# A hybrid attention kernel: last block's chain in halves, centred weights, two batches' residual kept by channels and added on GpSimd, run-up of 10 tokens

## The chip, the cores and the metric

The kernel runs on one core of a Trainium2 chip. A core has a matrix engine (TensorE, PE in the profile; PEld is its weight load), a vector engine (VectorE, DVE), a scalar engine (ScalarE, ACT), GpSimd (POOL), and SyncE (SP), which here only starts transfers (DMAs). The metric is device time in microseconds (us), lower is better; the figure for a kernel is the median over its runs.

## The reference

Four images (B = 4) of 128 channels (C) and 64 x 64 = 4096 tokens (N), in single precision. Layer 0 is an attention between tokens with 64-wide projections. Layer 1 normalizes each token, attends causally over 128 channels, adds the result, and then runs a recurrence over the tokens whose result is added once more. Cut to what the change touches:

```python
t = t + attention(layernorm(t))              # causal
# feed-forward part, on layernorm(t):
Wx = layernorm(t) @ W.T                      # (B, T, H)
Wx = (Wx - mean) * rsqrt(var + eps) * gamma + beta   # mean, var over all B*T tokens
y = 0
for each token:                              # lax.scan over T
    y = sigmoid(Wx[token] + y @ V.T)
    ys[token] = y
t = t + ys
```

The mean and variance of the batch norm are taken over all tokens of all images, so the recurrence can't start before the last block's Wx is there.

## The kernel before, in words

A first function, `fast_path`, does the work in a form that is valid under two conditions, which it checks at its end; a flag then decides whether a second, general path runs. On these inputs it is not meant to run.

**The main part.** Tokens are taken in blocks of 512 (BLK; NB = 8 blocks in an image), keys in tiles of 128. For each block and layer, a list of *items* is written out, an item being two tiles of keys: scores on PE into `s_ps` (L835 for layer 0, L844 for layer 1), exponential on ACT into `p` (L849, L851), sums for the denominator on DVE into `dsum` (L873, L875), and the weighted sum of values on PE into `acc` (L895, L903). A loop over *slots* issues in each slot the scores of one item, the values of the item two before, and one *task* from a list of waiting tasks: chains of small steps that finish a block are written as generators, which yield how many slots later their next step falls due. So the order on every engine is that of the slots.

**A block's end in layer 1** is the generator `finish1`. `first` divides by the denominators and adds to the residual stream `xs` (`joined`, L624), stores the resulting tokens in `x2` in DRAM, tokens by channels (L740), and takes mean and variance per token (`moments`: L633, L634, L636, and a power on GpSimd, L638). `norm` improves the inverse root by one Newton step (`newton`, L462 to L468) and normalizes (L645). `second` brings the normalized block into a layout with channels on partitions: for most blocks by a DVE transpose in squares of 32 (L659) and DMAs through DRAM (`by_c`, eventually `xhT`), for the very last block by PE transposes (L653) and one DVE copy (L654). `third` multiplies by W into `wx_ps` (L769), takes the statistics for the batch norm (L772) and copies the result over the block in `xs` (L782; L779 for the last block), arranged by steps of the recurrence.

**The last block of the last image** has its own order, since no other work lies beside it: all its steps follow in adjacent slots, and some matmuls without a use (`warm`, L730) are put between them. The function `form_half`, early in the kernel, prepares half of V's row sums (`v_half`, L486 to L489) right after `form` has prepared a product of weights `g1` (L491 to L494). Both take their PSUM tile from `misc`, a pool of two tiles that small products share.

**The recurrence.** The 4096 tokens of an image are cut into 256 chunks (NCH) of 16 tokens (STEPS), and all chunks run side by side as columns of one matmul. A chunk doesn't know the state that the chunk before it ends with; instead, it starts some tokens earlier (WARM = 11, the *run-up*) from a guess, so that its state at its first token is close to the true one. At the end the states at which run-ups ended are compared with the true ends of the chunks before (`gap`, L1109 to L1114, limit TOL = 1e-6). In each of the 11 + 16 steps, and for each of the four images: a matmul with V on PE (`y_ps`, L1077), a scale-and-add of Wx on DVE (`z`, L1079), and a sigmoid on ACT (L1082). The first of the run-up's steps needs no matmul: it is one activation with scale and `shift_half` (L1074). Scale and shift come from a chain of small operations on 128 x 1 tiles, L1036 to L1046.

**The output.** `x2` is loaded again into `xr` by 8 DMAs (L1033), with chunks on partitions. After the last step, `residual` transposes the states on PE into `yT_ps` (L1096), adds them to `xr` on DVE (L1098; four tokens of 128 chunks at a time, 32 in all), and stores 512 KB after each second addition (L1100, 16 DMAs). The states of the first four steps are kept in `early`; those of later steps lie in `xs`, in place of Wx.

Of the kernel before, what the change touches and what calls it, by code (L numbers as in the profile page):

```python
# [15 lines left out]
P = 128  # L16
BLK = 512
CHUNK = 1024
LN_EPS = 1e-5
BN_EPS = 1e-5  # L20


@with_exitstack
def general_path(
# [14 lines left out]
    out: bass.AP,  # L39
# [243 lines left out]
    with tc.tile_pool(name="wx", bufs=1) as wxp, tc.tile_pool(name="fwork", bufs=3) as wk:  # L283
# [28 lines left out]
        with tc.tile_pool(name="ys", bufs=3) as ysp, tc.tile_pool(  # L312
# [13 lines left out]
            for kb in range(nblk):  # L326
                ps = nxt
                y = ysp.tile([P, STEPS, B], F32, tag="y", name="y")
                for t in range(STEPS):
                    if prev is not None:  # L330
                        nc.tensor.matmul(
                            ps[:, t, :], lhsT=vf, rhs=prev, start=False, stop=t == STEPS - 1, skip_group_check=True
                        )
                    nc.scalar.activation(y[:, t, :], ps[:, t, :], AF.Sigmoid)
                    prev = y[:, t, :]
                    if t == STEPS // 2 and kb + 1 < nblk:
                        nxt = preload(kb + 1)
                o = ysp.tile([P, B, STEPS], F32, tag="o", name="o")
                nc.gpsimd.tensor_tensor(o, xs[:, :, ts(kb, STEPS)], y.rearrange("p t b -> p b t"), ALU.add)
                op = ps_o.tile([P, B, P], F32, tag="o", name="oT_ps")  # L340
                for b in range(B):
                    nc.tensor.transpose(op[:, b, :], o[:, b, :], ident)
                oT = ysp.tile([P, B, P], F32, tag="oT", name="oT")
                nc.vector.tensor_copy(oT, op)
                nc.sync.dma_start(out=out[:, ts(kb, STEPS), :].rearrange("b n c -> n b c"), in_=oT)
# [4 lines left out]
def fast_path(  # L350
# [15 lines left out]
    out: bass.AP,  # L366
# [14 lines left out]
    WARM, TOL, STEPS = 11, 1e-6, 16  # L381
# [14 lines left out]
    x2 = dram.tile([B, N, P], F32, name="x2")  # L396
# [40 lines left out]
    vf = const.tile([P, P], F32, name="vf")  # L437
    gamma = const.tile([P, 1], F32, name="gamma")
# [10 lines left out]
    ends = const.tile([P, 9], F32, name="ends")  # L449
# [3 lines left out]
    v_half = const.tile([P, 1], F32, name="v_half")  # L453
    spare = const.tile([P, 1], F32, name="spare")

    def rsqrt(y, var, z):

        nc.gpsimd.tensor_tensor(y, var, mhalf[:, : y.shape[-1]], ALU.pow)
        newton(y, var, z)

    def newton(y, var, z, pinned=False):
# [4 lines left out]
        nc.vector.tensor_tensor(z, z, var, ALU.mult)  # L466
        nc.vector.tensor_scalar(z, z, -0.5, 1.5, ALU.mult, ALU.add)
        nc.vector.tensor_tensor(y, y, z, ALU.mult)  # L468

    with tc.tile_pool(name="batch", bufs=1) as batch, tc.tile_pool(name="rows", bufs=2) as rowp, tc.tile_pool(  # L470
# [15 lines left out]
        def form_half():  # L486
            hp = misc("h_ps")
            nc.tensor.matmul(hp[:, 0:1], lhsT=vf, rhs=point5, start=True, stop=True)
            nc.vector.tensor_copy(v_half, hp[:, 0:1])  # L489
# [91 lines left out]

        def folded(den, by_pe):
# [7 lines left out]
            if by_pe:  # L590
# [4 lines left out]
                nc.vector.tensor_tensor(own, dp.rearrange("p (q j) -> p q j", q=Q), quarter, ALU.mult)  # L595
# [32 lines left out]
        def moments(b, g):  # L628
# [10 lines left out]
            return mv, var, y  # L639

        def normed(b, g, dst, mv, var, y, pinned=True):

            newton(y, var, stat.tile([P, TPB], F32, tag="z", name="ln_z"), pinned)
            for j in range(TPB):
                nc.vector.tensor_scalar(  # L645
# [75 lines left out]
        def finish1(b, g):  # L721
# [4 lines left out]
            def warm(n, rhs):  # L726

                ps = ps_s.tile([P, 2 * BLK], F32, tag="s", name="warm_ps")
                for _ in range(n):
                    nc.tensor.matmul(ps[:, : BLK // 2].rearrange("p (a c) -> p a c", c=P) if len(rhs.shape) == 3 else ps[:, : BLK // 2], lhsT=ident, rhs=rhs, start=True, stop=True)  # L730

            def first():
# [5 lines left out]
                if final:  # L738
                    warm(9, agg[:, : BLK // 2])
                nc.sync.dma_start(  # L740
                    out=x2[b, ts(g, BLK)].rearrange("(j p) c -> p j c", p=P),
                    in_=xs[:, b, ts(g, BLK)].rearrange("p (j c) -> p j c", c=P),
                )
# [3 lines left out]
            def norm():  # L747
                normed(b, g, mem["xh"], *mem["of"], not final)

            def second():  # L750
                mem["xhT"] = wk.tile([P, BLK], F32, tag="xhT2", name="xhT2")
                if final:
                    transposed(mem["xh"], mem["xhT"], "xh2T_ps", nc.vector.tensor_copy)
                    warm(1, mem["xh"][:, 2:])
# [11 lines left out]

            def third():
                wp = misc("wx_ps")
                nc.tensor.matmul(wp, lhsT=wf, rhs=mem["xhT"], start=True, stop=True)  # L769
                if b == B - 1 and g == NB - 1:  # L770
                    in_range(True)
                nc.vector.bn_stats(ends[:, 3:] if final else stats[:, b * NB + g], wp)  # L772
# [3 lines left out]

                to = xs[:, b, ts(g, BLK)]
                if final:
                    nc.scalar.copy(to.rearrange("p (s c) -> p s c", c=CPB), wp.rearrange("p (c s) -> p s c", s=STEPS))  # L779
                    warm(6, to[:, : BLK // 2])  # L780
                else:
                    nc.scalar.copy(  # L782
                        to.rearrange("p (s j q u) -> p s j q u", q=Q, j=TPB, s=STEPS),
                        wp.rearrange("p (q j u s) -> p s j q u", q=Q, j=TPB, s=STEPS),
                    )
# [13 lines left out]
            yield 2, second  # L799
            yield 1 if final else 6 if g < 2 or g == NB - 1 else 4, third  # L800
# [84 lines left out]
        def values(it):  # L885
# [24 lines left out]
            if it.last:  # L910
# [8 lines left out]
                else:  # L919
                    bt.agg = wk.tile([P, BLK], F32, tag="agg", name="agg")  # L920
                    nc.scalar.copy(bt.agg, bt.acc[:, 0])
# [102 lines left out]
    with tc.tile_pool(name="xr", bufs=1) as xrp, tc.tile_pool(name="y", bufs=2) as yp, tc.tile_pool(  # L1024
        name="ps_y", bufs=1, space=PSUM
    ) as ps_y, tc.tile_pool(name="ps_r", bufs=4, space=PSUM) as ps_r:

        HALVES = NCH // P
        by_chunk = lambda t: t.rearrange("b (h q s) c -> b h q s c", q=P, s=STEPS)
        xr = xrp.tile([P, B, HALVES, STEPS, P], F32, name="xr")  # L1030
        for b in range(B):
            for h in range(HALVES):
                nc.sync.dma_start(out=xr[:, b, h], in_=by_chunk(x2)[b, h])  # L1033
# [3 lines left out]
        scale = xrp.tile([P, 1], F32, name="scale")  # L1037
        var = xrp.tile([P, 1], F32, name="var")
        nc.vector.tensor_scalar(var, mv[:, 1:2], BN_EPS, None, ALU.add)
        rsqrt(scale, var, xrp.tile([P, 1], F32, name="z"))  # L1040
        nc.vector.tensor_tensor(scale, scale, gamma, ALU.mult)
        shift = xrp.tile([P, 1], F32, name="shift")
        nc.vector.tensor_tensor(shift, mv[:, 0:1], scale, ALU.mult)
        nc.vector.tensor_tensor(shift, beta, shift, ALU.subtract)
        shift_half = xrp.tile([P, 1], F32, name="shift_half")
        nc.vector.tensor_tensor(shift_half, shift, v_half, ALU.add)  # L1046
# [9 lines left out]

        assert HALVES * TPB == NB
        early = xrp.tile([P, B, TPB, NCH], F32, name="early")
        late = xs.rearrange("p b (r h k q) -> p b k r h q", h=HALVES, r=TPB, q=P)

        def states(b, s):
            return pair(early[:, b, s]) if s < TPB else late[:, b, s // TPB - 1, s % TPB]

        def step(b, s):

            wx = by_step[:, b, s % STEPS]
            if s == -1:
# [7 lines left out]
            else:  # L1075
                ps = ps_y.tile([P, NCH], F32, tag=f"y{b}", name="y_ps")
                nc.tensor.matmul(ps if s < 1 else pair(ps), lhsT=vf, rhs=prev[b], start=True, stop=True)  # L1077
# [4 lines left out]
                nc.scalar.activation(y, z if s < 0 else pair(z), AF.Sigmoid, bias=shift)  # L1082
            prev[b] = start[:, b, :NCH] if s == -1 else y

        for s in range(-WARM, STEPS):
            for b in range(B):
                step(b, s)

        def residual(b):

            for h in range(HALVES):
                for s0 in range(0, STEPS, TPB):
# [4 lines left out]
                    t = xr[:, b, h, ds(s0, TPB)]  # L1097
                    nc.vector.tensor_tensor(t, t, ps, ALU.add)  # L1098
                    if s0 % (2 * TPB):
                        nc.sync.dma_start(out=by_chunk(out)[b, h, :, part], in_=xr[:, b, h, part])  # L1100

        for b in range(B - 1):
# [4 lines left out]
        for b in range(B):  # L1107
            ps = ps_y.tile([P, NCH], F32, tag=f"y{b}", name="gap_ps")
            nc.tensor.matmul(pair(ps), lhsT=ident, rhs=prev[b], start=True, stop=False)  # L1109
# [72 lines left out]
```

## Time and profile before

| | us |
|---|---|
| median of the runs | 2064.52 (2064.33 to 2066.47, three runs) |
| profiled execution | 2065.22 |
| its span | 2063.5 |
| granted TensorE clock | 0.999 of full |
| main part, up to the last accumulation | 0 to 1974 |
| last block's chain and batch norm | 1974 to 1988 |
| recurrence | 1988 to 2036.6 |
| additions and output | 2036.6 to 2063.5 |

The span is what the profiler sees from the first to the last instruction; the execution's own time is 1.7 us longer. A line of the timeline gives the start, the length of the group (both in us), the engine and line, the operation with output and inputs and their shapes, how often it was run in the group, and in brackets how long the engine was idle before and which instruction ended that. A float32 matmul shows as two passes, so a count of 12 is six matmuls.

### The profile page before, as it was taken

The page shows a single profiled execution, that of the slowest core. Times are in us where ns is not written, and L with a number is a line of the kernel's source. Part 1 is how long each engine was busy: PE and PEld are TensorE (multiplying, and loading weights), DVE is VectorE, ACT ScalarE, POOL GpSimd, SP SyncE. Part 2 cuts the span into 40 slices and gives each one's busy share as a digit, 9 for nine tenths or more (in the row PEclk, how much of TensorE's full clock was granted, in tenths as well). Part 3 has the DMA queues.
Part 4 walks back from the last instruction along what each step waited for, and adds up shares of the span by engine and source line. Part 5 has one row for each costly group of instructions (what it writes and reads, how often), then busy time and mean ns, then how long its engine had stood idle before and what let it go on. Part 6 is the DMA issues. An engine that isn't in the chain of part 4 may idle for free.

```text
span 2063.5 us, 30798 instructions
## 1 busy us (share of the span) xinstructions
PE 2046.0 (99%) x11716; PEld 896.4 (43%) x11716; DVE 1492.2 (72%) x2865; ACT 990.1 (48%) x1071; POOL 135.5 (7%) x221
## 2 busy tenths in 40 slices
PE   9999999999999999999999999999999999999998
PEld 3333354444333345444333335544433334544456
DVE  4899867455889986644679987754588998764578
ACT  5666633323666643333466663332366664333365
POOL 1000011000000001000000001100000001100000
PEclk9999999999999999999999999999999999999999
DMA  4111012220100111231011101222000111110044
GB/s 113 43 23 23 12 42 51 69 67 16 57 8 17 23 28 46 62 77 41 17 43 22 23 12 42 47 67 72 16 17 5 19 23 28 41 43 25 16 169 165
DMA packets 207148, 89.03 MB, mean 43 GB/s; under 512 B 140960, under 2 KB 189600, under 8 KB 205968
## 3 DMA queue, kind: packets, MB, share of 16 engines
q1 hardware_dynamic: 205984, 86.42, 16.4%
q8 instruction: 94, 1.54, 0.3%
q14 instruction: 62, 0.51, 0.1%
q0 software_dynamic: 288, 0.39, 0.1%
q10 hardware_dynamic: 720, 0.16, 0.0%
HBM read 45.84 MB, written 36.89 MB: 40 GB/s over the span
## 4 chain that ended last, share of the span: by engine, by line
PE 97%; DVE 1%; issue 1%; DMA 0%; ACT 0%; POOL 0%; DVEq 0%; POOLq 0%; ACTq 0%
PE s_ps L844 22%; PE acc L903 22%; PE s_ps L835 22%; PE acc L895 21%; PE o_ps L614 3%; PE y_ps L1077 2%; PE r_ps L577 1%; PE wx_ps L769 1%; PE kr_ps L520 1%; PE v_ps L532 1%; DVE xr L1098 1%; PE warm_ps L484 0%; DMA swap<-kr 0%; ACT p L849 0%; DMA out_x<-xr 0%
## 5 line engine op out<-in xcount | busy, mean ns | idle before, releaser
L875 DVE TENSOR_TENSOR dsum<-dsum,p 128x1024 f32<-128x1024 f32 x676 | 826.0, 1222 | 430.2 <-ACT p L851 312.3
L849 ACT ACTIVATE p<-s_ps,nshift 128x1024 f32<-128x1024 f32 x512 | 569.6, 1117 | 315.0 <-PE s_ps L835 304.4
L851 ACT ACTIVATE p<-s_ps 128x1024 f32<-128x1024 f32 (+2 forms) x288 | 274.5, 953 | 605.5 <-PE s_ps L844 603.2
L895 PE MATMUL acc<-p,v 64*64 64x512 f32 x4096 | 529.2, 590 | 0.0
L835 PE MATMUL s_ps<-swap,kr 64*64 64x512 f32 x2048 | 524.1, 591 | 2.5 <-ACT p L849 1.6
L835 PE MATMUL s_ps<-kr 64*64 64x512 f32 x2048 | 524.1, 591 | 0.0
L844 PE MATMUL s_ps<-rows,xhT 128*128 128x512 f32 (+3 forms) x1152 | 502.9, 559 | 0.0
L903 PE MATMUL acc<-p,xh 128*128 128x512 f32 (+3 forms) x1152 | 500.8, 557 | 0.0
L903 PEld LDWEIGHTS acc<-p,xh 128*128 128x128 f32 x1152 | 216.2, 190 | 244.3 <-issue 233.5
L844 PEld LDWEIGHTS s_ps<-rows,xhT 128*128 128x128 f32 x1152 | 213.8, 190 | 242.4 <-issue 204.6
L895 PEld LDWEIGHTS acc<-p,v 64*64 64x64 f32 x4096 | 155.5, 133 | 281.7 <-issue 269.8
L835 PEld LDWEIGHTS s_ps<-swap,kr 64*64 64x64 f32 x2048 | 139.6, 133 | 141.1 <-issue 125.2
L835 PEld LDWEIGHTS s_ps<-kr 64*64 64x64 f32 x2048 | 139.7, 133 | 138.0 <-issue 133.8
L638 POOL TENSOR_TENSOR ln_rstd<-ln_var,mhalf 128x4 f32<-128x4 f32 x64 | 89.4, 1397 | 1102.1 <-DVE ln_var L636 1102.1
L883 DVE TENSOR_TENSOR dsum<-dsum,p 128x256 f32<-128x256 f32 (+1 forms) x120 | 54.9, 493 | 66.8 <-POOL p L855 66.8
L624 DVE SCALAR_TENSOR_TENSOR xs<-o_ps,recs,xs 128x128 f32<-128x128 f32 x256 | 75.0, 341 | 3.8 <-PE o_ps L614 0.5
L645 DVE TENSOR_SCALAR xh<-xs,ln_mv,ln_rstd 128x128 f32<-128x128 f32 x256 | 71.4, 342 | 2.2
L855 POOL TENSOR_SCALAR_AFFINE_SELECT p<-p 128x128 f32<-128x128 f32 x128 | 35.4, 300 | 466.6 <-ACT p L851 451.8
L633 DVE BATCH_NORM_STATS2 ln_st<-xs 128x6 f32<-128x128 f32 x256 | 63.3, 270 | 0.0
L782 ACT COPY xs<-wx_ps 128x512 f32<-128x512 f32 x31 | 18.1, 585 | 74.6 <-DVE stats L772 68.4
L873 DVE COPY dsum<-p 128x1024 f32<-128x1024 f32 x60 | 41.0, 684 | 12.1 <-ACT p L851 7.8
L1079 DVE SCALAR_TENSOR_TENSOR z<-xs,scale,y_ps 128x256 f32<-128x256 f32 x104 | 46.8, 480 | 2.9 <-PE y_ps L1077 1.7
(138 smaller groups left out, 984.6 us busy)
## 6 DMA issues: line engine op xcount, KB each, us to landing
xs<-in_xT SPq DMA_DIRECT2D x32, 256.0 KB, 2.9
by_r<-sqT SPq DMA_DIRECT2D x128, 64.0 KB, 2.2
xhT<-by_r SPq DMA_DIRECT2D x128, 64.0 KB, 2.0
x<-xs SPq DMA_DIRECT2D x32, 256.0 KB, 2.3
xr<-x SPq DMA_DIRECT2D x8, 1024.0 KB, 12.6
out_x<-xr SPq DMA_DIRECT2D x16, 512.0 KB, 4.7
by_c<-sqT SPq DMA_DIRECT2D x124, 64.0 KB, 1.8
xhT<-by_c SPq DMA_DIRECT2D x31, 256.0 KB, 2.6
```

The costliest lines, as they stand in the source:

```text
L614: nc.tensor.matmul(op[:, ts(j, P)], lhsT=agg[:, ts(j, P)], rhs=wv1 if layer else wo2, start=True, stop=True)
L624: nc.vector.scalar_tensor_tensor(t, in0=op[:, ts(j, P)], scalar=rec[:, j : j + 1], in1=t, op0=ALU.mult, op1=ALU.add)
L633: nc.vector.bn_stats(st[:, j], xs[:, b, ds(g * BLK + j * P, P)])
L638: nc.gpsimd.tensor_tensor(y, var, mhalf, ALU.pow)
L645: nc.vector.tensor_scalar(dst[:, j], xs[:, b, ds(g * BLK + j * P, P)], mv[:, j, 0:1], y[:, j : j + 1], ALU.subtract, ALU.mult)
L835: nc.tensor.matmul(ps[c * M : c * M + M, off : off + n], lhsT=bs[it.b].kr[part, h, ds(t % (NT // 2) * P + c * M, M)], rhs=rows[h], start=True,
L844: nc.tensor.matmul(ps[:, off : off + n], lhsT=lhsT, rhs=rhs, start=True, stop=True)
L849: nc.scalar.activation(it.p[:, :off], ps[:, :off], AF.Exp, bias=nshift)
L851: nc.scalar.activation(it.p[:, :off], ps[:, :off], AF.Exp, scale=float(P) ** -0.5)
L875: nc.vector.tensor_tensor(flat, flat, it.p, ALU.add)
L895: nc.tensor.matmul(bt.acc[h * M : h * M + M, r], lhsT=bt.v[part, t % (NT // 2), t // (NT // 2)], rhs=it.p[part, o : o + n], start=it.first ...
L903: nc.tensor.matmul(bt.acc[:, 0, q0:], lhsT=bt.xh[:, t], rhs=it.p[:, o : o + n], start=it.first and h == 0, stop=it.last and h == 1,)
```

## The change

- **Centred weights.** A matrix `center` (identity minus 1/128) times W gives `wfc`, whose product with a token doesn't depend on the token's mean. It is made in `form_half`, with a third PSUM tile from `misc` (`c_ps`). The last block is then only multiplied by its inverse root, and its mean isn't subtracted. `v_half` becomes `beta_half`, with beta added.
- **Halves.** For the last block the copy of `acc`, the normalization, the copy after the transposes, the product with W, the statistics and the copy into `xs` are done in two halves, some on ACT and some on DVE. An added dependency keeps the denominator's first operation behind DVE's half of the copy of `acc`.
- **Newton and scale chain.** The Newton step takes three operations instead of four, with -var/2 as an input; the scale and shift chain after the power takes fewer operations.
- **Two images by channels.** For images 0 and 1 (BY_C = 2) the residual stream isn't stored by tokens (`x2t` is for images 2 and 3 only). A new step `kept` transposes each of their blocks in squares on DVE and stores it by four DMAs in `x2c`, with channels on rows; it comes one slot after `second`. At the end `x2c` is loaded into `xc` (8 DMAs) and `x2t` into `xr` (4 DMAs).
- **Sums on GpSimd.** For these two images, after each of the 16 steps the states are added to `xc` by one GpSimd operation (128 x 512) and stored by one DMA of 256 KB (`out_c`). The kernel's output holds these images by channel, step and chunk, and the host puts them in order. `residual` runs for images 2 and 3 only.
- **Run-up.** WARM is 10 instead of 11, TOL 2e-6 instead of 1e-6.

```diff
-    WARM, TOL, STEPS = 11, 1e-6, 16
+    WARM, TOL = 10, 2e-6
...
-    def newton(y, var, z, pinned=False):
+    def newton(y, half, z, pinned=False):
         ins = nc.vector.tensor_tensor(z, y, y, ALU.mult)
...
-        nc.vector.tensor_tensor(z, z, var, ALU.mult)
-        nc.vector.tensor_scalar(z, z, -0.5, 1.5, ALU.mult, ALU.add)
-        nc.vector.tensor_tensor(y, y, z, ALU.mult)
+        nc.vector.tensor_tensor(z, z, half, ALU.mult)
+        nc.vector.scalar_tensor_tensor(y, in0=z, scalar=1.5, in1=y, op0=ALU.add, op1=ALU.mult)
...
             hp = misc("h_ps")
             nc.tensor.matmul(hp[:, 0:1], lhsT=vf, rhs=point5, start=True, stop=True)
-            nc.vector.tensor_copy(v_half, hp[:, 0:1])
+            nc.vector.tensor_tensor(beta_half, hp[:, 0:1], beta, ALU.add)
+            cp = misc("c_ps")
+            nc.tensor.matmul(cp[:, :P], lhsT=center, rhs=wf, start=True, stop=True)
+            nc.vector.tensor_copy(wfc, cp[:, :P])
...
+                if last:
+                    t = xs[:, b, ds(g * BLK + j * P, P)]
+                    if j % 2:
+                        nc.scalar.activation(dst[:, j], t, AF.Copy, scale=y[:, j : j + 1])
+                    else:
+                        nc.vector.tensor_scalar(dst[:, j], t, y[:, j : j + 1], None, ALU.mult)
+                    continue
...
-                    transposed(mem["xh"], mem["xhT"], "xh2T_ps", nc.vector.tensor_copy)
-                    warm(1, mem["xh"][:, 2:])
+                    for k, copy in enumerate((nc.vector.tensor_copy, nc.scalar.copy)):
+                        ps = misc("xh2T_ps")
+                        for i in range(2):
+
+                            nc.tensor.transpose(ps[:, ts(i, P)], mem["xh"][:, 2 * k + i], ident)
+                        copy(mem["xhT"][:, ts(k, BLK // 2)], ps[:, : BLK // 2])
...
+            def kept():
+
+                sq = squares(xs[:, b, ts(g, BLK)].rearrange("p (j c) -> p j c", c=P))
+                to = x2c[b, g].rearrange("r c (j q t) -> r c j q t", q=Q, t=S)
+                for q in range(Q):
+                    nc.sync.dma_start(
+                        out=to[:, :, :, q].rearrange("r c j t -> r (c j) t"),
+                        in_=sq[ts(q, S)].rearrange("r c j t -> r (c j) t"),
+                    )
...
+                to = xs[:, b, ts(g, BLK)].rearrange("p (s c) -> p s c", s=STEPS)
+                if final:
+                    in_range(True)
+                    for k in range(2):
+                        wp = misc("wx_ps")[:, : BLK // 2]
+                        nc.tensor.matmul(wp, lhsT=wfc, rhs=mem["xhT"][:, ts(k, BLK // 2)], start=True, stop=True)
+                        nc.vector.bn_stats(ends[:, 3 + 6 * k : 9 + 6 * k], wp)
+                        nc.scalar.copy(to[:, :, ts(k, CPB // 2)], wp.rearrange("p (c s) -> p s c", s=STEPS))
+                    warm(6, xs[:, b, ds(g * BLK, BLK // 2)])
+                    return
...
-                    nc.scalar.copy(bt.agg, bt.acc[:, 0])
+                    if it.b == B - 1 and it.g == NB - 1:
+                        nc.scalar.copy(bt.agg[:, : BLK // 2], bt.acc[:, 0, : BLK // 2])
+                        copied.append(nc.vector.tensor_copy(bt.agg[:, BLK // 2 :], bt.acc[:, 0, BLK // 2 :]))
+                    else:
+                        nc.scalar.copy(bt.agg, bt.acc[:, 0])
...
+        nc.gpsimd.tensor_tensor(y, var, mhalf[:, :1], ALU.pow)
+        nc.vector.tensor_scalar(half, var, -0.5, None, ALU.mult)
+        nc.vector.tensor_scalar(nmean, mv[:, 0:1], -1.0, None, ALU.mult)
+        nc.vector.scalar_tensor_tensor(z, in0=y, scalar=half, in1=y, op0=ALU.mult, op1=ALU.mult)
+        nc.vector.scalar_tensor_tensor(y, in0=z, scalar=1.5, in1=y, op0=ALU.add, op1=ALU.mult)
+        nc.vector.tensor_tensor(scale, y, gamma, ALU.mult)
+        nc.vector.scalar_tensor_tensor(shift_half, in0=nmean, scalar=scale, in1=beta_half, op0=ALU.mult, op1=ALU.add)
+        nc.vector.scalar_tensor_tensor(shift, in0=nmean, scalar=scale, in1=beta, op0=ALU.mult, op1=ALU.add)
...
+        def add(s):
+
+            t = sums.tile([P, BY_C, NCH], F32, tag="sum", name="sum")
+            by_grid = lambda t: t.rearrange("p b (g c) -> p b g c", c=CPB)
+            ins = nc.gpsimd.tensor_tensor(by_grid(t), by_step[:, :BY_C, s], by_grid(xc[:, :, :, s]), ALU.add)
+            tc.keep_in_program_order(ins)
+            tc.keep_in_program_order(nc.sync.dma_start(out=out_c[:, :, s].rearrange("b c k -> c b k"), in_=t))
...
         for s in range(-WARM, STEPS):
             for b in range(B):
                 step(b, s)
+            if s >= 0:
+                add(s)
...
-        for b in range(B - 1):
+        for b in range(BY_C, B - 1):
             residual(b)
```

The warming matmuls are also pinned to their place in the program's order (`keep_in_program_order`), and `warm` is called with 9 and 6 as before, the single one in `second` being left out.

## The prediction

> **What bounds the kernel now.** I read the shares by engine first, then the chain that ended last, then busy time by stretch, then the timeline of the tail. The page's share and chain:
>
> ```profile
> PE 2046.0 (99%) x11716; PEld 896.4 (43%) x11716; DVE 1492.2 (72%) x2865; ACT 990.1 (48%) x1071; POOL 135.5 (7%) x221
> ...
> PE 97%; DVE 1%; issue 1%; DMA 0%; ACT 0%; POOL 0%; DVEq 0%; POOLq 0%; ACTq 0%
> ```
>
> PE sets the time, but 99% is a mean. By stretch (columns: length, then busy us of PE, PEld, DVE, ACT, POOL, then granted clock, DMA share, GB/s):
>
> ```profile
> 30.00:1974.00 1944.00, 1942.38 (x11172) 827.32 (x11170) 1407.92 (x2668) 922.93 (x935) 127.97 (x198) 1.00 0.15 34
> 1974.00:1988.00 14.00, 10.87 (x48) 7.82 (x49) 8.10 (x42) 3.45 (x6) 1.66 (x3) 1.00 0.27 97
> 1988.70:2036.60 47.90, 47.90 (x220) 33.66 (x220) 46.78 (x105) 47.53 (x105) 0.00 (x0) 1.00 0.35 147
> 2036.60:2056.00 19.40, 17.65 (x135) 15.03 (x133) 19.32 (x35) 2.44 (x10) 0.00 (x0) 1.00 0.91 360
> ```
>
> Up to 1974 PE has no gap: other engines' work is free there, and only what holds PE costs. From 1974 to 1988 nobody is full: a serial chain (last block, then batch norm's scale). From 1988.7 the recurrence runs; DVE's scale-and-add (L1079) is 98% busy and each sweep of four batches takes four of them. From 2036.6 DVE's additions of the residual and the output DMA are both full. The timeline of those stretches:
>
> ```profile
> 1984.41 0.59 ACT L779 COPY xs<-wx_ps 128x512 f32<-128x512 f32 x1 [8.29 <-DVE ends L772]
> ...
> 1985.05 2.86 PE L730 MATMUL warm_ps<-xs,ident 128*128 128x256 f32 x12 [1.41 <-ACT xs L779]
> ...
> 1986.81 0.16 DVE L1046 TENSOR_TENSOR shift_half<-shift,v_half 128x1 f32<-128x1 f32 x1
> 1987.21 2.08 ACT L1074 ACTIVATE y<-xs,shift_half,scale 128x256 f32<-128x256 f32 x4 [2.21 <-DVE shift_half L1046]
> ...
> 1988.01 4.29 PE L1077 MATMUL y_ps<-y,vf 128*128 128x256 f32 x18
> ...
> 2036.52 14.43 DVE L1098 TENSOR_TENSOR xr<-xr,yT_ps 128x512 f32<-128x512 f32 x24
> ...
> 2037.82 18.46 SPq L1100 DMA_DIRECT2D out_x<-xr x16
> ```
>
> The warming matmuls (L730) end at 1987.91, the first y_ps starts at 1988.01: 1.04 after shift_half ends (1986.97). The recurrence's 104 scale-and-adds take 47.88 us (1988.72 to 2036.60): **0.460 each**, 1.84 a sweep. An addition takes 14.43/24 = 0.60; 32 last until 2055.92, and the last transfers and the drain need 7.6 more, to 2063.5.
>
> [...] GpSimd's power takes 1.01 us in the quiet tail and 1.91 beside L875, which adds two SBUF tiles (below). L1079 reads one SBUF tile and one PSUM tile, as L624 does, beside which an affine select took 294 ns, the same as alone.
> - [...] Here it fell about 4.5 us after PE's last work (2054.3); which shorter gap suffices isn't shown.
>
> ```profile
> 1941.07 1.91 POOL L638 TENSOR_TENSOR ln_rstd<-ln_var,mhalf 128x4 f32<-128x4 f32 x1 [23.96 <-DVE ln_var L636]
> ...
> 1978.39 1.01 POOL L638 TENSOR_TENSOR ln_rstd<-ln_var,mhalf 128x4 f32<-128x4 f32 x1 [7.04 <-DVE ln_var L636]
> ```
>
> **The change part by part** (line numbers of before, in us).
>
> 1. *Centred weights.* form_half gains a third PSUM tile (c_ps) in a pool of two. It waits until DVE has read the first, g_ps:
>
> ```profile
> 38.02 0.28 PE L488 MATMUL h_ps<-point,vf 128*128 128x1 f32 x2
> 38.12 1.23 DVE L875 TENSOR_TENSOR dsum<-dsum,p 128x1024 f32<-128x1024 f32 x1 [1.24 <-ACT p L849]
> 38.23 0.65 PE L835 MATMUL s_ps<-swap,kr 64*64 64x512 f32 x2
> ...
> 39.26 0.28 DVE L494 COPY g<-g_ps 128x128 f32<-128x128 f32 x1
> ```
>
> That copy stands behind an addition and ends at 39.54. In PE's built order s_ps and all that follows stand behind c_ps: 39.55 - 38.3 is 1.2, the matmul 0.2: **+1.4** on the bound engine. From 0 (other work is issued first) to +1.6.
>
> 2. *Chain of the last block.* Halving the copy of agg on ACT and DVE gains only 0.2: in the built order DVE's half waits for ACT's. Newton has one operation less: 0.2. From xh's start to the end of bn_stats is 4.15 now (1980.23 to 1984.38); with two xh each on ACT and DVE, copy, wx and statistics in halves, I work out 2.95: 0.65 until xh, 0.2 more for the transposes, 0.45 copy, 0.6 wx, then the second half's 0.6 wx and 0.4 statistics, partly overlapped: 1.2. After the batch norm's power there are 4 operations of 0.195 instead of 8: 0.8. Shift_half comes **2.4 earlier**, at 1984.55 (bounds 1.5 to 3).
>
> 3. *What the chain then meets.* In ACT's built order the first activation stands ahead of the two copies of wx into xs. The warming matmuls wait for both copies, and the first y_ps stands behind these matmuls on PE. Now the copy (1984.41) and the warming (1985.05) run under the scale chain; then they run after it: shift_half + 0.24 + 0.52 activation + 0.70 two copies + 0.05 + 2.96 matmuls = shift_half + 4.47, against + 1.04 now. First y_ps at 1984.55 + 4.47 = 1989.0 against 1988.0: **+1.0**. The chain's 2.4 is lost, and 1.0 more; the operations behind y_ps on every engine are the recurrence itself, so it all starts later by that. Bounds: -2.4 if the copies go first, +3.9 if in PE's 4 us without work (wx to warming) the clock halves, which doubles the 12 warming passes of 0.24.
>
> 4. *Run-up 10 for 11*: one sweep less, 4 x 0.460: **-1.84**.
>
> 5. *Keeping two batches' residual by channels.* Per block of batches 0 and 1, a DVE transpose (0.71 by L659) and four 64 KB DMAs take the place of one of 256 KB: 11.4 us of DVE and some 64 x 0.63 - 16 x 0.38 = 34 of SP, over 1,000 us. The cover is PE's matmuls; DVE has slack in each slot (10.98 of 12 us in a late stretch of layer 0). 0, bounds 0 to +2, if SP's longer queue delays a by_c or by_r whose reader PE is.
>
> 6. *Reading it back.* 12 DMAs instead of 8 for the same 8.4 MB; the first waits only for the last accumulation, as the last block's store does, which now stands behind it on SP. Even at half the full rate (400 GB/s in the tail) that ends by 2015, with the by-channel half (first in the queue) by 2000, ahead of the first sum (2009) and additions (2038). 0.
>
> 7. *Sums on GpSimd.* [...] one per sweep of 1.84: they lie beside the recurrence, with 256 KB written per sweep (142 GB/s). The last waits for batch 1's last sigmoid, ahead of the last scale-and-add[...]. Its store stands ahead of all the others' on SP, but the first of those has its two additions only 1.3 after: 0.
>
> 8. *After the recurrence.* 16 additions instead of 32: 16 x 0.60 + 0.6 (gap matmuls) = 10.2, then 7.6 as now: 17.8 from the last scale-and-add to the end, against 2063.5 - 2036.6 = 26.9: **-9.1**. By DMA: 4.45 MB at 400 GB/s is 11.1, and with start and drain 17.1, so DVE binds narrowly; -9.8 to -8.
>
> Sum: 1.4 + 1.0 - 1.84 - 9.1 = **-8.5**: span 2063.5 - 8.5 = 2055.0. Around the span lie 1.7 (the profiled execution took 2065.22), and that execution stands 0.7 over the median, 2064.52. So the median is **2056.0**.
>
> **Rivals.**
> - *The chain's gain arrives* (copies and c_ps cost nothing): -2.4 + 0 - 1.84 - 9.1 = -13.3, 2051.2. For it: everything PE waits for is short. Against: both waits follow from orders and buffers in the built program. In part (one of the two): 2053 to 2054.5. 12% for the two.
> - *The clock halves in PE's gap*: 12 x 0.24 = 2.9 more: 2058.9. [...] 18%.
> - *Main part disturbed by item 5*, +2 to +3: 2058.5. For: SP gets longer; against: PE's waits over the main part now sum to 1.6. 12%.
> - *GpSimd becomes the bound* (the slower side): if a sum takes d, the recurrence's last 16 sweeps end 16 x (d - 1.84) late; break-even at d = 1.84 + 8.5/16 = 2.37. [...] 7%.
> - *It doesn't do what it says*: the run-up of 10 misses the limit and the general path runs, far slower. The largest root gap worked out on the inputs is 1.0e-6, against 2e-6. 1%.
>
> The forecast's own case keeps 50%.
>
> **How the numbers follow.** Forecast 50%, faster rivals 12%, clock 18%, disturbed 12%, slower 8%. All but the last lie over 0.2% (4.1 us, about what a measurement can tell) below 2064.5, except that combined delays of item 5 and the clock may end within it: faster 0.84, same 0.08, slower 0.08. The range, 2050.8 to 2061.5, takes in the faster rival and the two delays together.
>
> **What would show it.** Right: y_ps first at about 1990.4 and after shift_half by 4.5; [...] 100 scale-and-adds of 0.46; 16 additions; 17.8 from the last one of the former to the end; one PE wait of 1.2 near 38. Wrong: GpSimd full from 2009 on, scale-and-adds longer than 0.46, or PE waiting on by_c or v.

## The result, and the profile after

The changed kernel takes **2059.45 us** in the median (2058.42 to 2060.53, nine runs), the kernel before, run beside it, 2064.71. The ratio is 0.9971, with an interval of 0.9962 to 0.9979: faster by 0.29%. The forecast was 2056.0, with a range of 2050.8 to 2061.5.

The page's shares by engine hardly differ, since the main part fills them:

```profile
PE 2039.1 (99%) x11646; PEld 909.0 (44%) x11646; DVE 1486.6 (72%) x2862; ACT 988.8 (48%) x1071; POOL 137.5 (7%) x237
```

By stretch, they differ at once (columns: length, busy us of PE, PEld, DVE, ACT, POOL, then clock, DMA share, GB/s):

```profile
1974.30:1985.00 10.70, 7.20 (x36) 5.67 (x36) 7.33 (x41) 2.93 (x6) 1.66 (x3) 1.00 0.83 191
1985.00:1992.00 7.00, 5.54 (x13) 3.93 (x13) 0.19 (x2) 2.61 (x6) 0.00 (x0) 0.54 1.06 204
1992.90:2039.00 46.10, 46.10 (x212) 32.69 (x211) 44.70 (x101) 44.99 (x100) 23.30 (x16) 1.00 0.56 189
2039.00:2050.40 11.40, 9.48 (x70) 8.29 (x68) 9.80 (x19) 2.39 (x10) 1.30 (x1) 1.00 0.85 330
```

The second line is new: 7 us in which DVE works 0.19, ACT 2.61, and PE is busy at a clock of 0.54. Of the recurrence only its first step, the activations that need no matmul, and the very first y_ps matmul fall into it. The last line is what was 19.4 long. The timeline of the changed kernel shows what fills the second line:

```profile
1984.84 0.22 DVE L1117 SCALAR_TENSOR_TENSOR shift_half<-nmean,scale,beta_half 128x1 f32<-128x1 f32 x1
...
1985.22 0.60 ACT L1150 ACTIVATE y<-xs,shift_half,scale 128x256 f32<-128x256 f32 x1 [3.61 <-DVE shift L1118]
1985.72 0.62 ACT L827 COPY xs<-wx_ps 128x256 f32<-128x256 f32 x2
1986.24 1.59 ACT L1150 ACTIVATE y<-xs,shift_half,scale 128x256 f32<-128x256 f32 x3
...
1986.40 5.49 PE L765 MATMUL warm_ps<-xs,ident 128*128 128x256 f32 x12 [3.78 <-ACT xs L827]
...
1991.94 6.38 PE L1153 MATMUL y_ps<-y,vf 128*128 128x256 f32 x26
...
1992.92 5.41 DVE L1155 SCALAR_TENSOR_TENSOR z<-xs,scale,y_ps 128x256 f32<-128x256 f32 x12 [7.73 <-PE y_ps L1153]
```

Read the brackets: PE had been idle for 3.78 when ACT's second copy let the warming matmuls go, and these took 5.49 for the 12 passes that took 2.86 before: 0.46 a pass against 0.24, at a granted clock of 0.50 against 1.00. The first y_ps follows them at 1991.94, 6.9 after shift_half.

**How two traces are laid on each other.** The first matmul of `g_ps` starts at 37.70 in the profile of before and at 36.61 in that of after. In the other profiles of this study it lies between 36.61 and 37.98, and nothing ahead of it differs by intent. That is spread of the start, of up to 1.4, and it blurs the comparison of single spans. So I count from this matmul, which I call the aligned time, and say so.

| stretch, us | before | after | difference | forecast |
|---|---|---|---|---|
| first g_ps to the copy of the last acc (1974.02, 1974.31) | 1936.32 | 1937.70 | +1.38 | +1.4 |
| to the first y_ps (1988.01, 1991.94) | 13.99 | 17.63 | +3.64 | +1.0 |
| to the end of the last scale-and-add (2036.60, 2038.94) | 48.59 | 47.00 | -1.59 | -1.84 |
| to the end of the span (2063.5, 2057.6) | 26.90 | 18.66 | -8.24 | -9.1 |
| sum | 2025.80 | 2020.99 | -4.81 | -8.5 |

### The profile page after: what moved, and what is told of

Its sections match the earlier page's. It is cut to its first block, busy times and chain, and to the rows that moved or that the text cites. A ratio compares the mean times of both kernels' runs of the same rounds, so it can differ in the third digit from the quotient of the medians.

```text
span 2057.6 us, 30790 instructions
## 1 busy us (share of the span) xinstructions
PE 2039.1 (99%) x11646; PEld 909.0 (44%) x11646; DVE 1486.6 (72%) x2862; ACT 988.8 (48%) x1071; POOL 137.5 (7%) x237
## 5 line engine op out<-in xcount | busy, mean ns | idle before, releaser
L951 PE MATMUL acc<-p,v 64*64 64x512 f32 x4096 | 543.0, 590 | 0.0
L891 PE MATMUL s_ps<-swap,kr 64*64 64x512 f32 x2048 | 538.9, 591 | 1.4 <-ACT p L905 0.9
L951 PEld LDWEIGHTS acc<-p,v 64*64 64x64 f32 x4096 | 166.6, 133 | 272.5 <-issue 251.6
L891 PEld LDWEIGHTS s_ps<-swap,kr 64*64 64x64 f32 x2048 | 151.4, 133 | 131.6 <-issue 107.8
L663 POOL TENSOR_TENSOR ln_rstd<-ln_var,mhalf 128x4 f32<-128x4 f32 x64 | 68.1, 1065 | 1099.5 <-DVE ln_var L661 1099.5
```

Of the source, the lines that this page charges most:

```text
L663: nc.gpsimd.tensor_tensor(y, var, mhalf, ALU.pow)
L891: nc.tensor.matmul(ps[c * M : c * M + M, off : off + n], lhsT=bs[it.b].kr[part, h, ds(t % (NT // 2) * P + c * M, M)], rhs=rows[h], start=True,
L951: nc.tensor.matmul(bt.acc[h * M : h * M + M, r], lhsT=bt.v[part, t % (NT // 2), t // (NT // 2)], rhs=it.p[part, o : o + n], start=it.first ...
```

## Experiments

The theory, in short: the gain of some 10 is made at the end (fewer additions and one sweep less), and half of it is lost in two places, in the queue order behind shift_half, which the halved clock makes dearer, and in the wait of `c_ps`. Its main rival: the halves themselves or GpSimd's sums are slow. All ratios are to the kernel before, run beside each variant.

### The copies ahead of the first activation (e1_copies_first)

```diff
-                nc.scalar.activation(grid(y), wx, AF.Sigmoid, scale=scale, bias=shift_half)
+                ins = nc.scalar.activation(grid(y), wx, AF.Sigmoid, scale=scale, bias=shift_half)
+                tc.keep_in_program_order(ins)
```

> Only the order on ACT changes: the four first activations are pinned behind the two copies of wx into xs. Theory (order): the copies run at about 1982.7 to 1983.5, the warming matmuls at 1983.5 to 1986.4 with the clock at full, first y_ps about 1986.5 instead of 1991.9; span 2057.6 - 5.5 - 0.3 (first sweep at full clock) = 2051.8, median about 2053.6, 0.9946 of before. Rival (the halved chain is itself late, or the clock falls in the shorter gap anyway): y_ps not before 1989, median 2056.5 or more. Second rival (GpSimd sums or the loads of xc and xr set the recurrence): no change, 2059.4.

Measured: 2054.54, ratio 0.9944 (0.9931 to 0.9958). Its timeline:

```profile
1984.07 0.76 ACT L827 COPY xs<-wx_ps 128x256 f32<-128x256 f32 x2 [1.12 <-DVE ends L826]
...
1984.88 2.86 PE L765 MATMUL warm_ps<-xs,ident 128*128 128x256 f32 x12 [0.93 <-ACT xs L827]
...
1986.55 2.08 ACT L1150 ACTIVATE y<-xs,shift_half,scale 128x256 f32<-128x256 f32 x4 [1.72 <-DVE shift L1118]
1987.85 8.36 PE L1154 MATMUL y_ps<-y,vf 128*128 128x256 f32 x36
```

One dependency, and PE's idle time falls from 3.78 to 0.93, the warming from 5.49 to 2.86, under the scale chain. From the copy of acc (1975.66) to the first y_ps it is 12.19, against 17.63: 5.4 less, as expected. The aligned span falls by 5.7, to 2015.3 (2053.3 - 37.98). The granted clock is 1.00 all the way from 1974 to 1996 here. The order was the loss, and with it the halved clock, which came with the gap of 3.78 and not with the one of 0.93.

### The halves undone, the rest kept (e2_no_halves)

```diff
-                    for k in range(2):
-                        wp = misc("wx_ps")[:, : BLK // 2]
-                        nc.tensor.matmul(wp, lhsT=wfc, rhs=mem["xhT"][:, ts(k, BLK // 2)], start=True, stop=True)
-                        nc.vector.bn_stats(ends[:, 3 + 6 * k : 9 + 6 * k], wp)
-                        nc.scalar.copy(to[:, :, ts(k, CPB // 2)], wp.rearrange("p (c s) -> p s c", s=STEPS))
+                    wp = misc("wx_ps")
+                    nc.tensor.matmul(wp, lhsT=wf, rhs=mem["xhT"], start=True, stop=True)
+                    nc.vector.bn_stats(ends[:, 3:9], wp)
+                    nc.scalar.copy(to, wp.rearrange("p (c s) -> p s c", s=STEPS))
...
-            cp = misc("c_ps")
...
```

> The last block's halves and the centred weights are undone (its mean is subtracted again, one copy of agg, one transpose copy, one wx, no c_ps), the rest of the change stays: shorter scale chain, three-operation Newton step, by-channel images, sums on GpSimd, run-up of 10. Theory (the halves cost what the tail gains): first y_ps near 1988.0 as before, bound by the warming matmuls that end at 1987.9; span 2063.5 - 1.8 - 8.2 = 2053.5, median about 2055.2, so 4 faster than the whole change. Rival (the halves help and the loss comes from elsewhere): slower than the whole change, 2060 or more.

Measured: 2054.23, ratio 0.9945 (0.9931 to 0.9958): without the halves the change is about 5 faster than with them. Here the copy runs ahead of the activation again. Two terms go: c_ps (below), and the late warming. But in the profiled execution (2055.5, the slowest of the five) the clock fell too, to a mean of 0.66 from 1984 to 1985 and 0.50 from there to 1987; whether it did in the others, no trace shows:

```profile
1983.18 0.59 ACT L809 COPY xs<-wx_ps 128x512 f32<-128x512 f32 x1 [8.08 <-DVE ends L808]
...
1983.82 4.54 PE L752 MATMUL warm_ps<-xs,ident 128*128 128x256 f32 x12 [1.41 <-ACT xs L809]
```

The gap is 1.41, the same as before, where these passes took 2.86 and the clock stayed at 1.00. So the length of the gap alone doesn't decide it; what does wasn't shown. It isn't that the halves are slow: from the copy of acc to shift_half's end it is 12.09 here (1972.99 to 1985.08) and 10.75 with them (1974.31 to 1985.06).

### No warming at that place (e3_no_warming)

```diff
-                    warm(6, xs[:, b, ds(g * BLK, BLK // 2)])
                     return
```

> The six warming matmuls after wx are left out of the changed kernel, all else stays, the order on ACT too. Theory (order and clock together): y_ps no longer stands behind them, it starts at shift_half + 0.24 + 0.6 + 0.05, about 1985.9, but PE has then been idle for 3.3; if the clock has halved, y_ps passes take 0.46 to 0.49 for some 5 us and PE, not DVE, sets these sweeps, 2 to 3 lost: span about 2054, median 2055.7. If the clock has not halved: span 2051.4, median 2053.1. Rival (warming wasn't on the path): unchanged, 2059.4 or slower.

Measured: 2055.64, ratio 0.9951 (0.9937 to 0.9964), as expected with the halved clock: it is 0.50 from 1986 to 1992. The view of DVE's and PE's timeline:

```profile
1986.29 10.03 PE L1152 MATMUL y_ps<-y,vf 128*128 128x256 f32 x30 [3.25 <-ACT y L1149]
...
1990.29 0.48 DVE L1154 SCALAR_TENSOR_TENSOR z<-xs,scale,y_ps 128x256 f32<-128x256 f32 x1 [0.37 <-PE y_ps L1152]
...
1991.14 0.48 DVE L1154 SCALAR_TENSOR_TENSOR z<-xs,scale,y_ps 128x256 f32<-128x256 f32 x1 [0.37 <-PE y_ps L1152]
```

y_ps starts at once, but at half clock its two passes take 0.85, and now DVE waits 0.37 for PE ahead of each scale-and-add, until 1992.7. The six late warming matmuls were worse than none.

### The centred weights' product four slots later (e4_c_ps_later)

```diff
+        def form_center():
             cp = misc("c_ps")
...
                     form_half()
+                    push(s, iter([(4, form_center)]))
```

> The centred weights' product is made four slots later instead of at once in form_half. Theory: PE's wait for DVE's copy of g near 38 us goes and with it the split of the s_ps group, the last accumulation ends 1.2 to 1.6 earlier, all that follows moves with it: median 2059.4 - 1.4 = 2058.0. Rival (the wait is made up for, since the next exponential was late anyway): within 0.3 of the whole change.

Measured: 2057.89, ratio 0.9960 (0.9947 to 0.9974), 1.6 under the changed kernel. The intervals of the two ratios overlap, so the traces have to decide: the aligned main part is 1936.49 instead of 1937.70, 1.2 less, as expected; most of the rest is that fewer warming passes ran at half clock in this profile (5.13 for the 12, and a mean clock of 0.74 from 1990 to 1991, where after's is 0.50). The changed kernel's timeline at c_ps:

```profile
36.61 0.49 PE L508 MATMUL g_ps<-wkT,wqT 128*128 128x128 f32 x2
...
37.03 1.23 DVE L931 TENSOR_TENSOR dsum<-dsum,p 128x1024 f32<-128x1024 f32 x1 [1.24 <-ACT p L905]
...
38.17 0.28 DVE L509 COPY g<-g_ps 128x128 f32<-128x128 f32 x1
...
38.51 0.49 PE L503 MATMUL c_ps<-wf,center 128*128 128x128 f32 x2 [0.30 <-DVE g L509]
```

The first block's copy of its accumulation follows 16.43 after g_ps in before, 18.21 in after, and 17.02 here: the product with its wait costs **1.78**, without the wait 0.59, so the wait alone 1.19. In the trace the wait is put at 0.3 only; one has to measure over the stretch, because half a group of s_ps was drawn ahead of it and ran unpaired: its two passes took 1.07 alone (at 37.14), where in before they and two others took 0.66 side by side (at 38.23).

### Each sum twice (e5_sums_doubled)

```diff
             tc.keep_in_program_order(ins)
+            ins = nc.gpsimd.tensor_tensor(by_grid(t), by_step[:, :BY_C, s], by_grid(xc[:, :, :, s]), ALU.add)
+            tc.keep_in_program_order(ins)
```

> Each GpSimd sum is issued twice (same inputs, same output), all else as in the changed kernel. Theory (the sums are hidden at 1.54 under a sweep of 1.84, GpSimd and the scale-and-adds do not exclude each other): a sweep's two sums take 3.1 to 3.4, GpSimd becomes the bound from 2011 on, its last sum ends near 2063 and the span grows by some 10 to 12 to about 2069, while the scale-and-adds stay at 0.46 each. Rival (GpSimd's reads hold up DVE): the scale-and-adds get longer than 0.46 as well. Second rival (the page's spans on GpSimd are too long): less than 5 more.

Measured: 2077.40, ratio 1.0059 (1.0043 to 1.0076). The groups of its sums and scale-and-adds:

```profile
L1165 POOL TENSOR_TENSOR sum<-xs,xc 128x512 f32<-128x512 f32 x16 | 24.6, 1535 | 25.5 <-ACT xs L1158 25.5
L1167 POOL TENSOR_TENSOR sum<-xs,xc 128x512 f32<-128x512 f32 x16 | 24.5, 1533 | 1.3
```

The second column of numbers is the mean in ns. GpSimd has hardly any idle time left between sums and ends at 2060.2 (2063 expected); the 100 scale-and-adds take 45.97, 0.460 each, so they don't meet. But I had expected 2069. What I missed is the order on SP:

```profile
2060.73 8.21 SPq L1189 DMA_DIRECT2D out_x<-xr  x8
```

All stores of the other two images stand behind the last sum's store, though their additions were done at 2051.2. They add 8 us after it.

### The sum on contiguous data (e6_sums_contiguous)

This kernel leaves the right sums out: it adds the values of other tokens, only to show what the stride costs. A sum took 1.54 in after, with xc read at a stride of 64 bytes; here xc is read in contiguous runs.

```diff
-by_grid(xc[:, :, :, s])
+by_grid(xc.rearrange("p b k s -> p b (k s)")[:, :, ts(s, NCH)])
```

> The sum reads xc in contiguous runs instead of every 16th element, so it adds values of other tokens and the output differs in these two images. [...] If it is the price of a two-input addition, it stays at 1.5. The time doesn't change in either case (within 0.5 of the changed kernel), since the sums are hidden.

Measured: 2059.74, ratio 0.9971 (0.9959 to 0.9982), no change in time. The sum's row here, and below it that of the changed kernel:

```profile
L1165 POOL TENSOR_TENSOR sum<-xs,xc 128x512 f32<-128x512 f32 x16 | 20.4, 1274 | 35.1 <-ACT xs L1158 32.8 <-POOL sum L1165 2.4
```

```profile
L1165 POOL TENSOR_TENSOR sum<-xs,xc 128x512 f32<-128x512 f32 x16 | 24.6, 1538 | 31.5 <-ACT xs L1158 28.6 <-DMA out_x<-sum 1.6 <-POOL sum L1165 1.3
```

So 0.26 of a sum is the stride's, and 1.27 is left without it.

### One image and three images by channels (e7_one_by_channel, e8_three_by_channel)

```diff
-BY_C = 2
+BY_C = 1      # e7; e8: 3
```

> Only one image by channels instead of two (BY_C = 1). Theory (DVE's additions set the tail): 24 additions instead of 16, 8 x 0.60 = 4.8 more from the last scale-and-add to the end, 23.5 instead of 18.7; median about 2064. Sums of 128x256 take about 0.8. Rival (the tail is set by the output transfers): 6.3 MB instead of 4.2 at 400 GB/s, 5.2 more, hardly to be told apart from it by the time, but then the additions would have idle time between them.

> Three images by channels (BY_C = 3). 8 additions are left, the sums are 128x768 and take 1.5 x 1.54 = 2.3, with 0.3 to the next 2.6, over the sweep of 1.84. Theory: GpSimd becomes the bound, its last sum ends at 2011 + 16 x 2.6 = 2053 and with the last store and drain the span is 2056 to 2058, no better than two images. Rival (tail falls by another 8 additions, GpSimd keeps up): 4.8 less, span 2053.

One image: 2061.48, ratio 0.9979 (0.9972 to 0.9986). From the last scale-and-add (2037.48) to the end (2060.2) it is 22.7, 4.1 more than with two; the additions run from 2037.39 to 2052.32 with one idle stretch of 0.21, which speaks for the theory, though the transfers have more to do as well. But the total rises by only 2.0, by the aligned spans 2.6 (2064 expected): the main part is 0.95 shorter (aligned 1936.75 to the copy of acc, against 1937.70), and the first y_ps comes 0.3 sooner after it. With three the main part is 0.91 longer (1938.61), and e12 below is 0.95 longer than e10. So **an image kept by channels takes 0.9 more of the main part than one kept by tokens**, which I had put at nothing.

Three images: 2061.42, ratio 0.9979 (0.9971 to 0.9987); the sums take 2.23, over the sweep of 1.84, and GpSimd is full, as expected, but only to 2045.7 and not to 2053. The aligned span is 0.9 above that with two: 0.91 more in the main part and 1.33 more after the last scale-and-add, less 1.36 in between, of which 1.15 is that the 12 warming passes took 4.34 here and 5.49 in after. But the fourth image's additions did not run meanwhile, as the theory has it. They stood behind a small operation of the flag's chain, and that one took 3.57 instead of 0.17:

```profile
2042.15 3.57 DVE L1202 TENSOR_SCALAR count<-gap 128x4 f32<-128x4 f32 x1 [3.54 <-ACT sq L1200]
```

It ends when GpSimd's last sum ends. To part the two causes I tried three images once more, after the edits of the next section (e12_three_mended: e10 with BY_C = 3).

> e10 with three images by channels. In e8 the fourth image's additions stood behind the small operation count, so GpSimd as the bound wasn't shown; here count stands behind them. Theory (GpSimd is the bound with three images): first sum at 2004.7, 16 sums of 2.23 end at about 2041, the additions by 2038; the last sum's store of 384 KB and the four of 512 KB behind it take 1 + 5.3, and some 4 of drain: 2051.5, with 0.9 for the third image in the main part 2052.4 for the span, 1.4 over e10; median about 2053.9. Rival (what held e8 up was count alone): 4 to 5 less than e10, 2048.

Measured: 2058.90, ratio 0.9970 (0.9959 to 0.9982), 6.4 slower than e10 and 5 slower than expected. Two rows of its timeline say why:

```profile
2010.16 34.61 POOL L1169 TENSOR_TENSOR sum<-xs,xc 128x768 f32<-128x768 f32 x16 [25.51 <-ACT xs L1162]
...
2037.78 7.01 DVE L1206 TENSOR_SCALAR count<-gap 128x4 f32<-128x4 f32 x1 [4.56 <-ACT sq L1204]
```

The sums begin at 2010.2 and not at 2004.7, where e10's begin; the loads of xc are 12 now, 6.3 MB, which at the 200 GB/s that the transfers reach from about 1979 on last until then. And count had been placed ahead of the additions again in the built order, in spite of its place in the program, and was now held for 7.01, until the sums' end (2044.77). So this run doesn't part the causes either: GpSimd is full to 2044.8 in any case, but what three images would take with the additions ahead of count stays open.

### All mended (e9_all_mended, e10_four_warming)

```diff
-        for b in range(BY_C, B - 1):
+        for b in range(BY_C, B):
             residual(b)
...
         nc.vector.tensor_scalar(flag, tp, P * (B + 2 * B * NT) - 0.5, None, ALU.is_lt)
-        residual(B - 1)
```

and the edits of e1 and e4; e10 also has `warm(4, ...)` for `warm(6, ...)`.

> Three edits on the changed kernel: the first activations pinned behind the copies (as in e1), the centred weights' product four slots later (as in e4), and the comparison of the run-ups' ends with its flag moved behind the last image's additions. Theory: the first two add up, -4.9 and -1.2 to -1.6, and the third takes the 1.5 us away that DVE waits for the last square in the middle of its additions, since the transfers still to come cover the flag: median 2059.4 - 4.9 - 1.4 - 1.5 = 2051.6. Rival (the tail is then set by the output transfers, which start no earlier): third edit worth less than 0.5, 2052.6 or more.

> As e9, with four warming matmuls instead of six. In e1 the warming ends at 1987.74, 0.67 after the first activation's end, so y_ps still waits for it. Theory: two fewer matmuls take that wait away, 0.7 less than e9, 2050.9. Rival: less work on PE lets the clock halve (as in e2, where it did with a gap of 1.4), and it is slower than e9 by 1 or more.

Measured: e9 2052.44, ratio 0.9936 (0.9922 to 0.9949), e10 2052.48, ratio 0.9933 (0.9920 to 0.9947). Both beat both kernels, by 0.65% against before. The third edit did what it says, but brought little. In after, DVE's additions had a hole:

```profile
2038.86 4.87 DVE L1184 TENSOR_TENSOR xr<-xr,yT_ps 128x512 f32<-128x512 f32 x8
...
2045.26 0.17 DVE L1202 TENSOR_SCALAR count<-gap 128x4 f32<-128x4 f32 x1 [1.53 <-ACT sq L1200]
```

In e9 it is closed:

```profile
2032.32 9.65 DVE L1188 TENSOR_TENSOR xr<-xr,yT_ps 128x512 f32<-128x512 f32 x16
...
2034.28 8.22 SPq L1191 DMA_DIRECT2D out_x<-xr  x8
```

Yet from the last scale-and-add (2032.41) to the end (2050.7) it is 18.3, only 0.4 less than in after: the trace is on the rival's side, that the output transfers set this tail. They begin 1.9 after the last scale-and-add, because the last sum's store (its sum ends at 2033.78) is ahead of them on SP, and run at some 400 GB/s, with the DMA engines over 90% busy from 2035 to 2045.

Between e9 and e10 the medians can't decide. By the traces, the time from the copy of acc to the first y_ps falls from 12.19 to 11.55, and the clock stays at 1.00 (1974 to 1996, in both); the aligned span falls by 0.6 (2013.7 to 2013.1).

### The run-up alone (e11_run_up_alone)

```diff
-    WARM, TOL, STEPS = 11, 1e-6, 16
+    WARM, TOL, STEPS = 10, 2e-6, 16
```

> The kernel before with a run-up of 10 and the limit 2e-6, nothing else. Theory: 4 scale-and-adds of 0.460 less, -1.84, median 2065.1 - 1.8 = 2063.3. Rival (the first sweeps are not bound by DVE, so one less saves less): -1.0 or less.

Measured: 2063.55, ratio 0.9990 (0.9982 to 0.9998). The scale-and-adds take 46.07 instead of 47.88, 1.81 less, as expected, and the aligned span falls by 1.8.

## Why the prediction was right, and where a term was off

The sign, the size within the range, and most of the mechanism held; the likeliest case did not. What happened is the forecast with its first delaying rival, the halved clock, which I had given 18% and 2058.9.

1. *Centred weights, +1.4*: the wait was there, as the buffers said, and cost the 1.2 foreseen; the product cost 0.59, not 0.2 (e4 and the first block's copy), 1.78 together. That the whole main part came out at +1.38 is luck (5).
2. *The chain, 2.4 earlier*: from the copy of acc to shift_half's end 10.75, against 12.95 before: 2.2.
3. *What the chain meets, +1.0*: **the step that was mis-sized.** The order was as foreseen, copies behind the activation, warming behind both, y_ps behind the warming, and e1 shows that it is the cause. But I worked with warming passes at full clock. At half clock these took 5.49 instead of the 2.96 that I summed, so the term was +3.64. My own bound for that case (+3.9) held. That it stood among the rivals, at 18%, was my estimate: the profile of before, the only one there was, shows no lower clock ahead of its end, where it fell at 2058.7, 4.4 after PE's last work, with nothing left to slow down. In the seven profiles that kept the order and the warming or left only the latter out (after, e3 to e8), PE's gap was 3.25 to 3.78. The clock fell to 0.50 in after, e3 and e4, and wherever the 12 passes were kept they took 4.34 to 5.49, against 2.86 in before; the term was then +2.5 to +3.6, so the profile of after is the dearest of its kind. As the slower passes came in all seven, the case belonged in the sum, not at 18%.
4. *Run-up, -1.84*: 1.81 (e11).
5. *Keeping by channels, 0*: 0.9 per image (e7, e8, e12) against an image kept by tokens. It didn't show in the sum, because something else in the change shortens the main part. From the copy of an image's first block to that of the next image's, the aligned times of after against before are +0.36 and +0.23 for the two images kept by channels and -0.98 for the third, kept by tokens; with the 1.77 of c_ps that makes the +1.38. About half of the 0.9 is a wait: where the next image's layer 0 begins, PE waits 0.44 to 0.46 for an exponential on ACT if the earlier image is kept by channels, 0.49 to 0.62 in before, and not at all if it is kept by tokens in the changed kernel. What takes that wait away there is open; I suppose the shorter Newton step, but no run took it alone.
6. *Reading back*: its transfers ran at 200 GB/s at first and were done by 2008, ahead of the first sum (2010.85); 0 held, with 3 to spare.
7. *Sums on GpSimd*: 1.54 each, which no row of before could show; that they would fit was an estimate of mine. They fit under the sweep of 1.84, and 0 held for the recurrence. But the last sum ends 1.4 after the last scale-and-add, and its store puts the first of the other images' stores off, from 1.2 after that scale-and-add (before) to 1.9. The slower rival did not occur: scale-and-adds take 0.460 beside sums that follow each other without a gap (e5), as they do with no sums in before. Its break-even, worked out from the sums' end alone, was too kind, for the other images' stores wait behind the sums' on SP.
8. *After the recurrence, -9.1*: -8.24. I had allowed 0.6 for the gap matmuls; DVE stood 1.53 for the last square in the middle of its additions. That it would have ended at 17.1 without (by DMA) was too short as well: e9 has 18.3, since the transfers begin only at 1.9.

## What to carry to other kernels

Before a serial chain is shortened, look at what stands in the queues behind its end: work that lay under the chain (here two copies and the warming) can come to lie behind it, and then the shorter chain is the slower one. A small product that takes a third tile from a pool of two waits for a reader on another engine, and so does everything behind it on its own (1.19 here); four slots later the wait was gone and only the product was left (0.59). And where one queue issues all stores, the order of the stores belongs to the price of any result that is stored.

## What the runs showed of the hardware

- The granted clock fell to 0.50 around gaps in PE's work in several profiles, but not after one fixed time. In the gap of 3.78 it fell 2.9 after the gap's start in after (at 1985.52) and about 1.6 after it in e4 (at about 1983.7); behind PE's last work it fell 4.4 later in before (at 2058.7) and 5.1 later in after (at 2053.8). In e2 the gap was 1.41, and the clock fell at about 1984.3, when PE had been at work again for half a us; in before and e11 the gap was 1.41 as well, and the clock stayed at 1.00. With gaps of 0.93 (e1, e9, e10, e12) it stayed at 1.00 too. In after it was full again at 1992.35, 6.83 after it fell, in e2 at about 1987.7. So neither the gap's length nor the time since its start tells these profiles apart, and what decides it wasn't shown. Rows of before (two), e2 (two) and after (two), with the columns of the result's section:

```profile
1984.00:1985.00 1.00, 0.00 (x0) 0.00 (x0) 0.76 (x4) 0.59 (x1) 0.12 (x1) 1.00 0.22 49
1985.00:1986.00 1.00, 0.95 (x4) 0.87 (x5) 0.47 (x3) 0.00 (x0) 0.42 (x1) 1.00 0.74 205
...
1984.00:1985.00 1.00, 1.00 (x4) 0.85 (x4) 0.68 (x4) 0.00 (x0) 0.18 (x1) 0.66 1.07 199
1985.00:1986.00 1.00, 1.00 (x3) 0.80 (x3) 0.21 (x2) 0.68 (x2) 0.00 (x0) 0.50 1.03 203
...
1985.00:1986.00 1.00, 0.00 (x0) 0.00 (x0) 0.19 (x2) 0.78 (x3) 0.00 (x0) 0.76 1.07 199
1986.00:1987.00 1.00, 0.60 (x2) 0.51 (x3) 0.00 (x0) 1.00 (x4) 0.00 (x0) 0.50 1.05 203
```

- A DVE operation on 128 x 4 elements (count) took 7.01 us (e12), 3.57 (e8) and 1.37 (e5) where GpSimd's sums followed each other, and 0.17 in after, where they had ended. In e5 it ended with the sum then running, in e8 and e12 only with the last of the row. The scale-and-adds beside the same sums in e5 took 0.460 each, as in before. What sets the two operations apart wasn't shown; no run changed the form of count. An operation of 0.17 held up the additions behind it until the sums' end (e8, e12).
- A two-input addition on GpSimd of 128x512 took 1.27 contiguous (e6) and 1.54 with one input at a stride of 64 bytes (after); 128x256 took 0.86 (e7) and 128x768 2.23 (e8), both strided. From these three sizes I estimate 0.69 for each further 256 and some 0.17 fixed.
